# Products that nobody reads, issued in TensorE's waits at the end of a two-layer transformer block

## The chip, the cores and the metric

The kernel runs on one core of a Trainium2 chip. The metric is the device time of one execution in microseconds (us), the median of several runs. A core has a matrix engine (TensorE, PE in the profile; its weight loads stand apart as PEld), VectorE (DVE), ScalarE (ACT), GpSimd (POOL) and SyncE (SP, which issues most DMAs). Each engine works through its own list of instructions in order and waits on semaphores for the others. The profile also gives the TensorE clock that the chip granted, as a share of full speed.

## The reference

The input x is 2048 tokens of 256 values; a context of 1601 rows of 256 goes with it. Every step is added to x:

```python
x = x + cross_attention(layernorm(x), ctx, tau, delta)     # 16 heads of 16
x = x + experts(layernorm(x))                              # top 1 of 8, gated
x = x + local_attention(ctx, layernorm(x), slen, pt)       # a window around pt
x = x + slots(layernorm(x))                                # 64 slots
```

The last of them is what matters here. For every token it computes `h = gelu(x @ w1 + b1)`, logits over 64 slots, the 8 largest and a softmax over these (`alpha`). Then all tokens are summed into the slots (`slot_input = alpha.T @ x`, divided by the sum of alpha), a GRU cell updates the slots, they attend to each other, are normalized and projected, and `out = alpha @ slot_values` goes back to the tokens. So everything after `slot_input` needs all tokens, is small (64 rows), and is one chain.

## The kernel before

**Stages.** The first 820 us or so are the projections and the cross attention. Then come the experts in five blocks of tokens, `BLOCKS`: three of 512 tokens (four tiles of 128), two of 256. For each block, `experts(lb)` (line 1024 for the products, 1031 for VectorE's gated sums) is TensorE's main load. Beside it run generators, which are called a step at a time: `front(lb + 1)` (norm and router of the next block), `windowed(lb)` (the local attention of a finished block: lines 1179 to 1215) and `weights(lb)` (the slots' alpha of a finished block: lines 1297 to 1345). A `yield` ends a step, and the next step of another generator follows in the program.

**The order of work.** The order of instructions on every engine is the order in which the Python code emits them; the section is under `tc.manual_schedule()`, and no scheduler moves them. In the loop over blocks, `aside(3)` takes three steps of these generators behind each pair of experts. After the last block no experts are left, and

```python
    while beside:
        aside(1)
```

empties the generators that remain: the local attention and alpha of the last two blocks. This is called the flush here. What it emits: `normed` (L96 and L98 statistics on VectorE, L102 on GpSimd for 1/std, L107 the normalization, L984 transposes on TensorE, L987 copies on ScalarE), then for the window L1179 (`s_ps`), L1188 (exp), L1198 (`t_ps`), L1207 and L1211 (`o_ps`), L1213 (tanh), L1215 (the sum into x, on GpSimd); for the weights L1292 (a bias into x, on GpSimd), L1297 (`h_ps`), L1299 (gelu), L1303 (`l_ps`), L1307 to L1328 (logits, the 8 largest, softmax, alpha, nearly all on VectorE), L1335 (`si_ps`, the sum into the slots), L1341 (`at_ps`, alpha turned), L1343 and L1345 (its two parts `aT`).

**The slots' chain** follows the flush: L1390 to L1393 (`den`, `si`), L1399 (`siT`, turned), L1419 (`rz_ps` and `in_ps`), L1423 to L1434 (gates, tanh, the new state `sn`), L1399 (`snT`), L1442 and L1448 (q, k, v), L1452 (`qk_ps`), L1454 to L1461 (softmax), L1463 (`pt_ps`), L1467 (`sc_ps`), the norm (L96 to L107), L1399 (`yT`), L1475 and L1477 (`s_ps`), L1482 and L1483 (its two parts), and at last, for eight pairs of token tiles, L1492 (`f_ps`), L1498 (the sum `o`, on VectorE, three buffers) and L1499 (the DMA to the output).

**Products and records.** A float32 matmul stands in the trace as two records (two passes), a transpose, a float32r and a bfloat16 matmul as one. `xnT` is a float32 tile [128, 2, 512] that was last read by the experts of the first block. `y_pool` has four PSUM buffers, which the experts' products use in turn.

## Time and profile before

| what | value |
|---|---|
| median of 3 runs | 1109.17 us (1107.79 to 1112.33) |
| the profiled execution's own time | 1109.3 us |
| its span, first to last instruction | 1107.5 us |
| mean granted TensorE clock | 0.935 |
| TensorE busy | 970.1 us (88%) |
| VectorE busy | 744.4 us (67%) |
| ScalarE busy | 516.6 us (47%) |
| GpSimd busy | 71.9 us (6%) |

The span is what the trace covers; the execution's own time is 1.8 us longer. A busy time is the time in which an engine has at least one instruction in work. All positions in the text are us from the start of the span. The last expert product of the program ends near 1027, the flush reaches from about 1031 to 1071, the slots' chain from there to 1095, and the output to the end.

### The profile page before, as it was taken

Reading aid. Unit: us, or ns where it says so; the run is one execution under the profiler, and the core shown is the slowest. Engines: PE = TensorE matmul, PEld = TensorE weight load, DVE = VectorE, ACT = ScalarE, POOL = GpSimd, SP = SyncE. Lnnn points to the kernel's source line nnn. Section 1 sums busy time; section 2 is a strip of 40 time slices with the busy share of each in tenths; the row PEclk is TensorE's granted clock in tenths of the full one; section 3 lists DMA queues with packets and bytes.
Section 4 is the critical chain, followed back from the end, with each engine's and each line's share of the span. In section 5 each row is a group of like instructions: output and inputs, shape, how many; then the busy total and the mean of one; then the engine's idle time right before and its main releaser. Section 6 shows DMA issues by size and latency. Waiting matters only on the chain.

```text
span 1107.5 us, 14588 instructions
## 1 busy us (share of the span) xinstructions
PE 970.1 (88%) x5647; PEld 445.1 (40%) x5647; DVE 744.4 (67%) x1431; ACT 516.6 (47%) x614; POOL 71.9 (6%) x96
## 2 busy tenths in 40 slices
PE   5787879999888999988899999989979999989755
PEld 2243323344333344443344444344334454545523
DVE  6455857888676888776788877867025658586644
ACT  2323545666555666655466675656830012121420
POOL 4001100000010000000000000000030002111210
PEclk9676989999999999999999999989998999999767
DMA  4845630310103000102110010100051000000002
GB/s 167 171 120 115 118 113 1 104 28 1 27 2 112 28 1 27 28 1 70 43 28 23 6 28 1 27 2 1 2 168 51 1 1 1 0 1 1 1 0 76
DMA packets 32275, 46.95 MB, mean 42 GB/s; under 512 B 6411, under 2 KB 21268, under 8 KB 31950
## 3 DMA queue, kind: packets, MB, share of 16 engines
q1 hardware_dynamic: 30478, 43.65, 14.8%
q10 hardware_dynamic: 1232, 1.61, 0.4%
q8 instruction: 44, 0.72, 0.3%
q0 software_dynamic: 496, 0.76, 0.3%
q14 instruction: 25, 0.20, 0.1%
HBM read 26.77 MB, written 14.04 MB: 37 GB/s over the span
## 4 chain that ended last, share of the span: by engine, by line
PE 63%; DVE 27%; issue 5%; DMA 2%; ACT 1%; SPq 1%; POOL 1%; POOLq 0%; DVEq 0%; ACTq 0%
PE acc L832 18%; DVE mx L267 16%; PE a_ps L263 11%; PE s_ps L876 11%; PE y_ps L1024 6%; PE a_ps L240 2%; DVE xn L107 2%; DVE x_sb L1031 2%; DVE ln_stats L96 1%; PE a_ps L807 1%; PE o_ps L1207 1%; PE a_ps L510 1%; PE a_ps L293 1%; PE x_ps L473 1%; PE si_ps L1335 1%
## 5 line engine op out<-in xcount | busy, mean ns | idle before, releaser
L267 DVE TENSOR_REDUCE mx<-a_ps 128x1 f32<-128x402 f32 (+1 forms) x661 | 489.1, 782 | 130.5 <-PE a_ps L263 126.0
L881 ACT ACTIVATE es<-s_ps 128x1024 f32<-128x1024 f32 (+1 forms) x416 | 406.0, 1021 | 249.8 <-PE s_ps L876 230.0
L263 PE MATMUL a_ps<-kb,qb 50*128 50x402 bf16 x992 | 214.6, 347 | 35.2 <-DVE mx L267 12.0
L876 PE MATMUL s_ps<-qt,kt 52*128 52x512 f32 (+1 forms) x832 | 233.1, 518 | 2.1 <-DMA qt<-nT 2.1
L832 PE MATMUL acc<-es,v 128*32 128x512 f32 (+1 forms) x1664 | 229.8, 624 | 0.0
L263 PEld LDWEIGHTS <-qb 50*128 50x128 bf16 x1024 | 75.8, 95 | 300.3 <-issue 283.1
L876 PE MATMUL s_ps<-ql,kt 52*128 52x512 f32 (+1 forms) x832 | 187.6, 400 | 0.0
L876 PEld LDWEIGHTS s_ps<-qt,kt 52*128 52x128 f32 (+1 forms) x832 | 89.2, 187 | 50.4 <-ACT es L881 27.3
L876 PEld LDWEIGHTS s_ps<-ql,kt 52*128 52x128 f32 (+1 forms) x832 | 99.3, 189 | 0.4
L1024 PE MATMUL y_ps<-expert_wT_sb,xT 128*128 128x512 f32 x192 | 90.7, 605 | 0.0
L1031 DVE SCALAR_TENSOR_TENSOR x_sb<-y_ps,r_gate,x_sb 128x256 f32<-128x256 f32 x96 | 46.3, 482 | 32.9 <-PE y_ps L1024 31.2
L102 POOL TENSOR_TENSOR ln_rstd<-ln_ve,mhalf 128x2 f32<-128x2 f32 (+2 forms) x28 | 21.1, 754 | 714.5 <-DVE ln_ve L100 714.5
L832 PEld LDWEIGHTS acc<-es,v 128*32 128x32 f32 (+1 forms) x1664 | 33.3, 109 | 49.7 <-issue 48.1
L1024 PEld LDWEIGHTS y_ps<-expert_wT_sb,xT 128*128 128x128 f32 x192 | 34.6, 192 | 32.4 <-issue 30.8
L987 ACT COPY xT<-tr_ps 128x512 f32<-128x512 f32 (+1 forms) x28 | 13.5, 493 | 61.2 <-PE tr_ps L984 61.1
L781 DVE RECIPROCAL rec<-a_ps 128x16 f32<-128x16 f32 x16 | 4.1, 258 | 52.0 <-PE a_ps L240 52.0
L107 DVE TENSOR_SCALAR xn<-x_sb,ln_mv,ln_rstd 128x256 f32<-128x256 f32 x64 | 31.6, 539 | 1.1 <-POOL ln_rstd L102 1.1
L1024 PE MATMUL y_ps<-expert_wT_sb,xnT 128*128 128x512 f32 x64 | 32.0, 623 | 0.0
L984 PE MATMUL tr_ps<-ident,xn 128*128 128x128 f32 x88 | 17.8, 303 | 9.6 <-DVE xn L107 9.6
L1031 DVE SCALAR_TENSOR_TENSOR x_sb<-y_ps,gate,x_sb 128x256 f32<-128x256 f32 x32 | 15.5, 483 | 14.0 <-PE y_ps L1024 13.4
L96 DVE BATCH_NORM_STATS2 ln_stats<-x_sb 128x6 f32<-128x256 f32 x64 | 23.4, 413 | 1.8 <-POOL x_sb L1215 1.8
L267 DVE TENSOR_REDUCE mx<-s_ps 128x2 f32<-128x804 f32 x16 | 15.9, 994 | 12.5 <-PE s_ps L263 12.5
(341 smaller groups left out, 710.5 us busy)
## 6 DMA issues: line engine op xcount, KB each, us to landing
qt<-q_rows SPq DMA_DIRECT2D x32, 192.0 KB
q_rows<-qhi SPq DMA_DIRECT2D x8, 512.0 KB
qb<-q_rows SPq DMA_DIRECT2D x30, 96.0 KB
kt<-expert_wT_sb SPq DMA_DIRECT2D x24, 100.5 KB
q_rows<-qp SPq DMA_DIRECT2D x8, 256.0 KB
q_rows<-qlo SPq DMA_DIRECT2D x8, 256.0 KB
ql<-q_rows SPq DMA_DIRECT2D x32, 64.0 KB
expert_wT_sb<-in_expert_wT SPq DMA_DIRECT2D x1, 2048.0 KB
```

The costliest lines, as they stand in the source:

```text
L96: nc.vector.bn_stats(stats[:rows, i, :], src[:, i, :])
L102: nc.gpsimd.tensor_tensor(rstd[:rows, :n], ve[:rows, :n], mhalf[:rows, :n], ALU.pow)
L107: nc.vector.tensor_scalar(dst[:, i, :], src[:, i, :], mv[:rows, i, 0:1], rstd[:rows, i : i + 1], ALU.subtract, ALU.mult,)
L240: nc.tensor.transpose(ps[:, t * P : (t + 1) * P], src[:, t, c * P : c * P + n], ident)
L263: nc.tensor.matmul(ps[:, k, :CH], qb[u % 2][rows, pl, t * P : (t + 1) * P], kb[g][rows, pl, c * CH : (c + 1) * CH], start=True, stop=True,)
L267: nc.vector.tensor_reduce(flat[:, n : n + m], ps[:, :m, :CH], AX.X, ALU.max)
L832: nc.tensor.matmul(acc[HP * j : HP * (j + 1), :], v[:n, i, h * VW : h * VW + HP], es[j // 2][:n, j % 2, :], start=i == 0, stop=i == NS - 1,)
L876: nc.tensor.matmul(ps[:n, h, :], kt[u % NG][rows, pl, i * P : i * P + n], q[u % nq][rows, pl, :], start=k == 0, stop=k == 1,)
L881: nc.scalar.activation(e[:n], ps[:n], AF.Exp)
L984: nc.tensor.transpose(ps[:, t * P : (t + 1) * P], xn[:, t, c * P : (c + 1) * P], ident)
L1024: nc.tensor.matmul(ps.rearrange("p e d -> p (e d)"), xT[:, c, tok], ew[:, c, pair * 2 * D : (pair + 1) * 2 * D], start=c == 0, stop=c == 1,)
L1031: nc.vector.scalar_tensor_tensor(xb[:, t, :], ps[:, k, :], gate[:, t, e : e + 1], xb[:, t, :], ALU.mult, ALU.add,)
```

## The change

A helper `busy(n)` is added. It emits n bfloat16 products, each with its weight load: 128 columns of the upper halves of `xnT`'s float32 values as weights, 512 columns of such halves as the moving operand (every second bfloat16, thus a step of 4 bytes). All write the same PSUM tile, `busy_ps`, which nothing reads; none waits for another engine once that buffer is free. `busy` does nothing until `calm` holds that tile, and it gets it right before the flush. So products are emitted from there on alone: 95 of them, at places in `normed`, `windowed`, `weights` and the slots' chain. On TensorE they stand in the program's order: 8 ahead of the first `h_ps` and 6 behind it, 4 and 4 around the second transposes of the next blocks, 2, 4 and 3 around the next `s_ps` and `l_ps`, 4 ahead of `t_ps`, 4 ahead of `o_ps`, 8 behind it, 2 ahead of the last transposes, 2 ahead of the last `l_ps`, 12 behind it, 6 behind the last `at_ps`, 12 behind `in_ps`, 5 behind `qk_ps`, 9 behind `sc_ps`. All other instructions keep their order on every engine.

```diff
--- before
+++ after
@@ -961,6 +961,16 @@
     BLOCKS = [(0, TPB), (TPB, TPB), (2 * TPB, TPB), (3 * TPB, 2), (3 * TPB + 2, 2)]
 
+    calm = []
+
+    def busy(n):
+
+        for _ in range(n if calm else 0):
+            nc.tensor.matmul(
+                calm[0].rearrange("p e d -> p (e d)"), xnT[:, 1, :P].bitcast(BF16)[:, 1::2],
+                xnT[:, 0, :].bitcast(BF16)[:, 1::2], start=True, stop=True,
+            )
+
@@ -973,10 +983,12 @@
         for t in range(0, nt, 2):
             stats.append(layer_norm_stats(xb[:, t : t + 2], 2))
+            busy(4)
             yield
         for t in range(0, nt, 2):
             for k in range(2):
                 layer_norm_apply(xb[:, t : t + 2], xn[:, t : t + 2], k, stats[t // 2])
+            busy(2)
             yield
@@ -1192,6 +1204,7 @@
         nc.vector.tensor_tensor(sc, sc, sm.to_broadcast(full), ALU.mult)
+        busy(3)
         yield
@@ -1297,6 +1310,7 @@
         nc.scalar.activation(hT[:, : nt * P], ps, AF.Gelu, bias=b1)
+        busy(2)
         yield
@@ -1312,11 +1326,13 @@
             nc.vector.match_replace(rest[:, t, :], mx8[:, t, :], lg[:, t, :], -3e38)
+        busy(4)
         yield
 
         nc.vector.tensor_tensor(rest, rest, lg, ALU.not_equal)
         nc.vector.tensor_tensor(lg, lg, mx8[:, :, 0:1].to_broadcast(full), ALU.subtract)
         nc.scalar.activation(lg, lg, AF.Exp)
+        busy(4)
         yield
@@ -1329,6 +1345,7 @@
             sm.unsqueeze(2).to_broadcast(two_of), ALU.mult,
         )
+        busy(4)
         yield
@@ -1383,9 +1400,11 @@
+    calm.append(y_pool.tile([P, 2, D], F32, tag="y", name="busy_ps"))
     while beside:
         aside(1)
 
+    busy(6)
     den = slot.tile([NSLOT, 1], F32, name="den")
@@ -1419,6 +1438,7 @@
                 ps, siT[:, c, :], wih[:, c, span], start=c == 0, stop=c == 1
             )
+    busy(12)
     rz = brz
@@ -1450,6 +1470,7 @@
     nc.tensor.matmul(ps, qk[0], qk[1], start=True, stop=True)
+    busy(5)
     nmx = slot.tile([NSLOT, 1], F32, name="nmx4")
@@ -1465,6 +1486,7 @@
     nc.tensor.matmul(ps, paT, v4, start=True, stop=True)
+    busy(9)
     y = slot.tile([NSLOT, 1, D], F32, name="y4")
```

## The prediction

> **What bounds the kernel now.** I read the page's forty slices first, because the change adds work only at the end.

> ```profile
> PE 970.1 (88%) x5647; PEld 445.1 (40%) x5647; DVE 744.4 (67%) x1431; ACT 516.6 (47%) x614; POOL 71.9 (6%) x96
> ...
> PEclk9676989999999999999999999989998999999767
> ```

> TensorE is busy 88% of the span, but the last three slices (83 us) have a granted clock of 0.7, 0.6 and 0.7, where most others have 0.9 and more. Next I cut the end into stretches of 3.41 us, the grain in which the clock changes. Columns: stretch, length, busy us of PE, PEld, DVE, ACT and POOL with instructions, granted clock, DMA share, GB/s.

> ```profile
> 1031.22:1034.63 3.41, 2.54 (x10) 1.06 (x10) 3.05 (x12) 2.56 (x3) 1.69 (x3) 1.00 0.00 0
> 1034.63:1038.05 3.42, 1.36 (x11) 1.05 (x11) 3.16 (x4) 0.37 (x1) 3.42 (x3) 1.00 0.00 0
> 1038.05:1041.46 3.41, 2.47 (x9) 2.02 (x9) 3.20 (x14) 1.59 (x4) 0.85 (x1) 0.50 0.00 0
> ...
> 1048.29:1051.70 3.41, 3.41 (x12) 2.14 (x11) 0.67 (x5) 0.30 (x1) 0.00 (x0) 0.50 0.02 5
> 1051.70:1055.11 3.41, 2.75 (x14) 2.08 (x13) 2.45 (x7) 1.46 (x4) 0.00 (x0) 1.00 0.00 0
> 1055.11:1058.53 3.42, 1.41 (x6) 0.63 (x6) 1.20 (x6) 0.37 (x1) 1.97 (x2) 1.00 0.00 0
> 1058.53:1061.94 3.41, 2.91 (x8) 1.86 (x8) 1.10 (x3) 2.03 (x3) 1.27 (x1) 0.50 0.01 2
> ...
> 1079.01:1082.42 3.41, 0.31 (x2) 0.20 (x2) 2.33 (x7) 1.70 (x2) 0.00 (x0) 1.00 0.00 0
> 1082.42:1085.83 3.41, 3.22 (x14) 1.89 (x14) 1.05 (x5) 0.00 (x0) 0.00 (x0) 0.50 0.01 2
> 1085.83:1089.25 3.42, 0.88 (x3) 0.29 (x3) 1.78 (x7) 0.40 (x2) 0.00 (x0) 1.00 0.00 0
> ```

> Read each line's PE time against the clock of the *next*. At full clock, 2.75 of 3.41 (81%) and 2.54 (74%) keep it; 1.36 (40%), 1.41, 0.31 and 0.88 halve it. At half clock, 3.41 and 3.22 (94%) restore it; 2.47 (72%) and 2.91 (85%) don't. So 48 of the last 70 us run at half clock, after four waits. TensorE's waits of the end:

> ```profile
> PE tr_ps L984 <- DVE xn L107: 5.4, 3, 2.4
> PE si_ps L1335 <- DVE alpha L1328: 5.3, 3, 4.0
> PE snT_ps L1399 <- DVE sn L1434: 3.2, 1, 3.2
> PE l_ps L1303 <- ACT hT L1299: 2.5, 3, 1.1
> PE yT_ps L1399 <- DVE y L107: 2.5, 1, 2.5
> ```

> (Total us, times, longest.) TensorE waits for a chain over VectorE, ScalarE and GpSimd, then works slowly itself while they wait. The same `si_ps` matmuls in the timeline (start, us):

> ```profile
> 1055.07 1.08 PE L1335 MATMUL si_ps<-xn,alpha 128*64 128x257 f32 x4 [0.66 <-DVE alpha L1328]
> 1068.06 1.97 PE L1335 MATMUL si_ps<-xn,alpha 128*64 128x257 f32 x4 [4.05 <-DVE alpha L1328]
> ```

> Four records take 1.08 us at full clock and 1.97 at half.

> [...]the line lies between 41% and 74% here. [...]The trace has no such product. Its nearest row is the float32r `f_ps` (L1492), which reads 4 bytes per column as the strided product does: its 256 columns start 0.213 us apart at half clock and 0.113 to 0.123 at full, [...]a step of 4 bytes is no obstacle. [...]I take **0.216 us** a product; the lower end is 0.213, the upper 0.43[...].

> **The change, part by part.** Nothing is removed or moved, no DMA is added and no other engine's list changes; a product waits for nobody. Its cost is what it holds up on TensorE; its gain is the clock. If no stretch falls to 41%, all of 1038 to 1099 runs at full clock.

> Costs and gains along the path, before minus after:

> - 1031 to 1046.6. The 14 products around the first `h_ps` (3.0 us) make `l_ps` end near 1037.5 instead of 1035.5. Its reader, L1307, stands behind the normalization L107, which crawls beside GpSimd's L1292 until 1039.06: hidden. From 1039.11 to 1043.87 the PE work halves (4.76 to about 2.4) and takes in ten products (2.2): even. `l_ps` then waits for gelu, behind two table loads (cover for the next four), and alpha is VectorE's (cover for three): **0**.
> - 1046.63 to 1051.70 is PE work without a wait at half clock: 5.07 becomes 2.54, plus the eight products around `t_ps`, 1.73, which nothing hides: **0.8**.
> - Eight products behind `o_ps` end near 1055.3; alpha's `si_ps` starts 0.25 late, ends with `at_ps` and two more products near 1057.2, before `xn` at about 1057.7: **0**, beside tanh, L1215, the statistics and L102.
> - `tr_ps` to `h_ps`, 1.32 to 1.07: **0.25**. `h_ps` to gelu 2.11; afterwards the table load ends last, 0.31 + 1.28 behind `h_ps`' start: 1.6, **0.5**. `l_ps` to L1307, 1.15 to 0.64: **0.5** (the two products lie under gelu).
> - The twelve behind `l_ps`, 2.6 us, lie under VectorE's 4 us to alpha: **0**. `si_ps`, `at_ps`, L1343, L1345 to `den` took 3.47; the two PE parts lose 0.95 and 0.35: **1.3**. The six (1.3) lie under L1343 to L1393 (wait 1.8): **0**.
> - `siT`: **0.1**. `rz_ps` 3.67 to 1.85: **1.8**. L1427 waited for `in_ps` until 1079.06, 2.05 behind L1423; then for the sigmoid, 1.4: **0.6**. The twelve (2.6) lie under the gates, 3.2 before `snT`: **0**.
> - `snT` was at full clock. q, k, v and `qk_ps`, 3.2 to 1.85: **1.35**. Five products, 1.1, under the softmax's 1.4; nine, 1.94, under the norm's 2.5: **0**.
> - `yT` and `s_ps`, 1090.87 to 1094.47, 3.6 to 1.95: **1.65**. First `f_ps` group to `o`, 1.53 to 1.05, then VectorE's 0.69 a group and the output's 2.2 us DMA set the pace: **0.6**.

> Sum 0.8 + 0.25 + 0.5 + 0.5 + 1.3 + 0.1 + 1.8 + 0.6 + 1.35 + 1.65 + 0.6 = 9.45 us. From the profiled execution's 1109.3 (span 1107.5 and 1.8 around it; 0.13 above the median of 1109.17) that leaves 1099.85, so 1099.7 for the median. I say **1100.0**.

> **Rivals.**

> *The clock still drops once or twice.* The thinnest stretches left are those with `si_ps` and the transposes before 1060 (I count about 53% busy) and the one after 1037. Against: 53% lies above every stretch that dropped in the end of before. For: between 41% and 74% the lines above tell nothing. A drop costs half of 3.4 us of path work, 1.7, plus its products at twice the length, some 0.7. One or two take 2.4 to 4.8 from the gain: about 1103.

> *Slower: the products outlast the waits.* One mechanism: a product takes 0.43 us, because the strided read needs two cycles or because the clock isn't lifted by them. With the clock lifted, the flush's beginning then overruns its cover: 14 products are 6 us, and the eight between the transposes 3.4 where 2.4 were freed, about 4 us late at alpha. Add 3.4 around `t_ps`, and overruns of 1.1 (12 in 4.05), 0.8 (6 in 1.8), 1.9 (12 in 3.2), 0.7 (5 in 1.4) and 1.3 (9 in 2.5): 13.2. Against this stands a gain of 9.45 + 1.73 = 11.2: 2 us slower, 1111. If the clock isn't lifted at all, the cost is about 7 with no gain: 1116. The sign turns near 0.4 us a product. The `f_ps` starts speak against the first form; every restored stretch in the lines above having been full of real products speaks against the second.

> *No difference.* The clock is set by something else in this stage[...], or the products are undone. Their place in TensorE's list is that of the source, so the change does what it says; 1109.

> **How the numbers follow.** Forecast 0.58, dropped clock 0.22, no difference 0.10, slower 0.10. A measurement of this kernel tells about 0.5% (5.5 us) from no change, so faster means below 1103.6: the forecast and half of the dropped clock, 0.69, rounded to 0.70; same is the other half and no difference, 0.21, rounded to 0.20; slower 0.10. The range runs from 1097.5 (products that cost nothing around `t_ps`, 1.7 more gain, and rounding) to 1107, which takes in two or three drops; the other cases, 0.2, lie outside.

> **What would show it.** The clock is 1.00 in every stretch from 1031 to the output's start. `rz_ps` takes 1.9 us instead of 3.67, its neighbours likewise. The product's row has starts 0.216 apart and about 20 us in all. TensorE's waits before `si_ps`, `snT` and `yT` shrink to under 1.5 us and still end with VectorE; where the releaser of real work becomes a product, my covers are wrong. Starts 0.43 apart at clock 1.00 would make the slower rival true, a clock of 0.50 beside products the second form of it.

## The result

The changed kernel takes 1104.24 us (median of 20 runs, 1097.44 to 1108.69) against 1112.61 us (20 runs, 1107.58 to 1122.07) for the kernel before on the same chip. The ratio is **0.9918, 95% interval 0.9896 to 0.9939**. The forecast, 9.45 us of 1109.3, is a ratio of 0.9915. The kernel is faster, by as much as was said. In microseconds it lies above the forecast of 1100.0, mostly because the kernel before took 1112.61 here and not the 1109.17 that the forecast started from.

The page of the changed kernel answers the two lines shown of before. First TensorE's busy time and its number of matmuls, then the granted clock in forty slices:

```profile
PE 981.9 (89%) x5738; PEld 446.6 (40%) x5742; DVE 744.5 (67%) x1431; ACT 516.6 (47%) x614; POOL 71.9 (7%) x96
...
PEclk8676898999999999999999999998998989999999
```

The last three slices stand at 0.9 now. The trace holds 91 records of the 95 products; VectorE, ScalarE and GpSimd do the same work as before.

The profiled span is only 2.5 us shorter (1105.0 instead of 1107.5), because in that execution the flush began 6.44 us later, at 1037.56 instead of 1031.12. The part ahead of it is the same code in both, but spent a different time at half clock: 95.6 us ahead of the flush in the trace before, 109.2 in the trace of the changed kernel. So I compare the **tail**, from the flush's first `tr_ps` to the end of the last `o`: 72.95 us before, 64.02 after, 8.93 less. The tails of all kernels below are measured this way.

The stretches of 3.41 us that answer to those of before (stretch, length, busy us of PE, PEld, DVE, ACT and POOL with instructions, granted clock, DMA share, GB/s):

```profile
1037.13:1040.54 3.41, 3.35 (x16) 1.82 (x16) 2.53 (x10) 2.01 (x3) 1.84 (x2) 1.00 0.00 0
...
1043.96:1047.37 3.41, 2.29 (x14) 1.28 (x13) 3.27 (x11) 1.03 (x4) 1.44 (x2) 1.00 0.00 0
...
1071.26:1074.67 3.41, 2.08 (x10) 1.02 (x10) 1.23 (x5) 0.55 (x3) 0.00 (x0) 1.00 0.00 0
...
1081.50:1084.91 3.41, 2.48 (x18) 1.27 (x16) 1.92 (x6) 1.13 (x1) 0.00 (x0) 1.00 0.02 5
```

None of the stretches from here to the output's start is at 0.50. The thinnest has TensorE busy for 2.08 of 3.41 us (61%), around the wait for `alpha`, and keeps the clock. TensorE's longest waits of the end, in the changed kernel (total us, times, longest):

```profile
PE tr_ps L996 <- DVE xn L107: 2.1, 3, 1.0
PE si_ps L1352 <- DVE alpha L1344: 1.7, 2, 1.3
...
PE snT_ps L1418 <- DVE sn L1454: 0.5, 1, 0.5
...
PE yT_ps L1418 <- DVE y L107: 0.4, 1, 0.4
```

They are what is left behind the products: 4.0 became 1.3 before `si_ps`, 3.2 became 0.5 before `snT_ps`. The releaser is still VectorE, so the products lie under work that ended last anyway. The profile names a product as releaser once, for the weight load of the last `tr_ps` (1.5 us). That product ended near 1063.9 and the load started at 1064.84, and the transpose's own wait ends with `xn`, so no cover failed there. The timeline of TensorE shows it step by step (start, us, and in brackets the idle time ahead):

```profile
1068.51 2.88 PE L969 MATMUL busy_ps<-xnT 128*128 128x512 bf16 x12
1072.71 1.08 PE L1352 MATMUL si_ps<-xn,alpha 128*64 128x257 f32 x4 [1.33 <-DVE alpha L1344]
...
1076.67 1.93 PE L1438 MATMUL rz_ps<-WihT_sb,siT 128*64 128x512 f32 x4 [0.38 <-DVE siT L1423]
```

The last `si_ps` takes 1.08 us, where it took 1.97, and `rz_ps` 1.93, where it took 3.67.

### The profile page after: what moved, and what is told of

It is laid out like the page before. It is cut to its first block, busy times and chain, and to the rows that moved or that the text cites. A ratio compares the mean times of both kernels' runs of the same rounds, so it can differ in the third digit from the quotient of the medians.

```text
span 1105.0 us, 14775 instructions
## 1 busy us (share of the span) xinstructions
PE 981.9 (89%) x5738; PEld 446.6 (40%) x5742; DVE 744.5 (67%) x1431; ACT 516.6 (47%) x614; POOL 71.9 (7%) x96
## 4 chain that ended last, share of the span: by engine, by line
PE 63%; DVE 28%; issue 4%; DMA 2%; ACT 1%; SPq 1%; POOL 1%; POOLq 0%; DVEq 0%; ACTq 0%
PE acc L832 19%; DVE mx L267 16%; PE a_ps L263 11%; PE s_ps L876 10%; PE y_ps L1036 7%; DVE xn L107 2%; DVE x_sb L1043 2%; PE a_ps L240 2%; PE a_ps L510 1%; DVE ln_stats L96 1%; PE a_ps L807 1%; PE o_ps L1220 1%; PE a_ps L293 1%; PE x_ps L473 1%; PE a_ps L473 1%
## 5 line engine op out<-in xcount | busy, mean ns | idle before, releaser
L102 POOL TENSOR_TENSOR ln_rstd<-ln_ve,mhalf 128x2 f32<-128x2 f32 (+2 forms) x28 | 21.1, 753 | 709.8 <-DVE ln_ve L100 709.8
L107 DVE TENSOR_SCALAR xn<-x_sb,ln_mv,ln_rstd 128x256 f32<-128x256 f32 x64 | 31.8, 543 | 1.1 <-POOL ln_rstd L102 1.1
L969 PE MATMUL busy_ps<-xnT 128*128 128x512 bf16 x91 | 23.5, 387 | 0.4 <-issue 0.2
```

Source lines behind the costliest of these rows:

```text
L107: nc.vector.tensor_scalar(dst[:, i, :], src[:, i, :], mv[:rows, i, 0:1], rstd[:rows, i : i + 1], ALU.subtract, ALU.mult,)
L969: nc.tensor.matmul(calm[0].rearrange("p e d -> p (e d)"), xnT[:, 1, :P].bitcast(BF16)[:, 1::2], xnT[:, 0, :].bitcast(BF16)[:, 1::2], start ...
```

## The experiments

Ten kernels were run. "Restored" means that the clock goes from half to full, "dropped" the other way. Where a ratio is given, it is to the kernel before on the same chip.

**Only the flush, and only the chain.** Is the gain a sum of local ones, or does the chain need the products of the flush to hand it a full clock? In flush_only the four calls of the chain, 32 products, go:

```
-    busy(6)
     den = slot.tile([NSLOT, 1], F32, name="den")
...
-    busy(12)
     rz = brz
...
-    busy(5)
     nmx = slot.tile([NSLOT, 1], F32, name="nmx4")
...
-    busy(9)
     y = slot.tile([NSLOT, 1, D], F32, name="y4")
```

In chain_only the list stays empty until the flush is over, so its 63 products go:

```
-    calm.append(y_pool.tile([P, 2, D], F32, tag="y", name="busy_ps"))
+    hold = (y_pool.tile([P, 2, D], F32, tag="y", name="busy_ps"))
     while beside:
         aside(1)

+    calm.append(hold)
     busy(6)
```

> The 63 products of the flush stay, the 32 of the slots' chain (6, 12, 5, 9) are left out. I measure the tail: from the start of the transposes ahead of the first h_ps of the flush to the end of the last sum o; it was 72.9 us in the profile before and 64.0 in the changed kernel's. Theory (a 3.4 us stretch that is about 40% busy halves the clock, one over 90% busy restores it): full clock through the flush, then it drops in the wait for snT (3.2 us without a product) or already at siT, and q, k, v and from yT to f_ps run at half clock: 1.35 + 1.65 + 0.5 us lost, tail 67.5, up to 70 if it drops at siT. Rival (each product helps only where it stands, so the chain's whole share goes): the stages from siT on lose all their 6.0 us, tail 70.0. Rival (the clock has nothing to do with it): clock pattern as in the profile before.

> The 32 products of the slots' chain stay, the 63 of the flush are left out. Theory: four half-clock stretches as before from about 1038 to 1051 and from 1058 on; the six products ahead of siT run at half clock, 2.6 us against a wait of 1.8, so siT comes 0.8 late, but they fill the array, and the clock is restored within one or two stretches, during rz_ps; from snT on all is at full clock. Gain 1.35 + 1.65 + 0.5 and about half of 2.4, less 0.8: tail about 69. Rival (each product helps only where it stands): all of the chain's 6.0 us, tail 66.9.

flush_only: tail 69.79, ratio 0.9982 (0.9965 to 1.0000). Its stages in the flush are those of the changed kernel within 0.05 us; from there on the clock drops. Its stretches at the beginning of the chain:

```profile
1067.29:1070.70 3.41, 1.24 (x7) 0.54 (x6) 1.50 (x5) 1.66 (x2) 0.00 (x0) 1.00 0.00 0
1070.70:1074.12 3.42, 3.42 (x5) 0.95 (x5) 0.00 (x0) 0.00 (x0) 0.00 (x0) 0.50 0.00 0
```

Without the six products the wait for `si` leaves TensorE busy for 36% of a stretch, and the next, which holds `rz_ps`, runs at half clock:

```profile
1069.84 0.34 PE L1417 MATMUL siT_ps<-ident,si 64*128 64x64 f32 x2 [1.79 <-DVE si L1411]
1070.56 3.56 PE L1437 MATMUL rz_ps<-WihT_sb,siT 128*64 128x512 f32 x4 [0.38 <-DVE siT L1422]
```

chain_only: tail 68.83, ratio 0.9963 (0.9943 to 0.9982). The flush is as before, and `siT` comes 0.07 us later than before; from `rz_ps` on, every stage has the changed kernel's length. The six products behind the last `si_ps` restored the clock, and I had the chain lose more of its gain. The tail hides that, because one output transfer came late in this trace. TensorE's last four matmuls waited for `o`, and `o` for the buffer of a transfer:

```profile
DVE o L1521 <- DMA out_x<-o: 4.3, 3, 2.1
```

The stage from the first `f_ps` to the end took 10.62 us instead of 8.63. Why that transfer was late stays open, and so does whether it is late in most executions: the ratio's interval allows a gain of 2.0 to 6.3 us, which holds both cases. Without its 2.0 us the tail is 66.8, as the rival had it. The tail of flush_only fits the upper end of the theory (70) as well as the rival (70.0), so it is chain_only that tells them apart. Each half brings what its own stages are worth: 3.2 us in flush_only, and in chain_only 4.1, or 6.1 without the late transfer; with that, 9.3 in two parts against 8.9 together. So the idea that the chain needs a full clock handed on from the flush falls: six products restored it here.

**Short products.** Are the products themselves what helps, as instructions in the list, or the work that they give TensorE? The same 95 products with 64 columns instead of 512:

```
-    calm[0].rearrange("p e d -> p (e d)"), xnT[:, 1, :P].bitcast(BF16)[:, 1::2],
-    xnT[:, 0, :].bitcast(BF16)[:, 1::2], start=True, stop=True,
+    calm[0].rearrange("p e d -> p (e d)")[:, :64], xnT[:, 1, :P].bitcast(BF16)[:, 1::2],
+    xnT[:, 0, :64].bitcast(BF16)[:, 1::2], start=True, stop=True,
```

> All 95 products stay at their places, with 64 columns of the moving operand instead of 512 (about 0.05 to 0.11 us each). Theory (share of busy time): the waits are filled to no more than a half of what they were, the long ones (before si_ps, snT, yT) stay under 41% busy, and the clock drops there: at least three half-clock stretches, tail 70 to 73. Rival (that TensorE gets an instruction now and then is enough): full clock throughout, tail 62 to 63, since the products that nothing hides cost less.

Tail 71.76, ratio 1.0000 (0.9979 to 1.0021). The products fill too little of the waits; the clock still drops, five times in the tail:

```profile
1041.52:1044.94 3.42, 3.42 (x18) 2.81 (x17) 2.69 (x15) 2.60 (x6) 0.00 (x0) 0.50 0.02 5
1044.94:1048.35 3.41, 1.53 (x17) 1.28 (x16) 2.54 (x8) 3.33 (x4) 0.00 (x0) 1.00 0.00 0
1048.35:1051.76 3.41, 3.40 (x8) 1.66 (x8) 2.17 (x12) 0.00 (x0) 0.00 (x0) 0.50 0.00 0
```

A full stretch at 0.50 (3.42 us busy) restored the clock, one that was 45% busy (1.53, with 17 matmuls) dropped it. So the number of instructions brought little: 1.2 us of the 8.9. Whether it is the time that they fill or the columns that they move, this run doesn't tell; one_row below adds the rows.

**Twice the products.** Do the waits have room, and does the cost come back where they have none?

```
-        for _ in range(n if calm else 0):
+        for _ in range(2 * n if calm else 0):
```

> Each place has twice the products (190). Tests the price of a product and the covers. Theory: full clock throughout; each place's second half at 0.226 us each is compared with the wait that the changed kernel's profile still shows there: about 4.9 us late at the second si_ps stage, 1.8 around t_ps, 1.3 behind o_ps, 1.4 at the twelve before si_ps, 0.9 at siT, 2.2 at snT, 0.9 at pt_ps, 1.65 at yT: 15 us in all, tail 79, slower than before by some 5 us. Rival (products give way to real work that is ready): tail 64 to 66.

Tail 77.95, ratio 1.0087 (1.0058 to 1.0117), no stretch at half clock. The stages that the forecast had covered are full now: the first, to `si_ps`, takes 20.10 us instead of 15.52, and that from `pt_ps` to `yT_ps` 5.28 instead of 3.70. The products didn't give way to real work. The tail's 5.0 us over before make a ratio of 1.0045; the rest up to the lower end of the interval, 1.4 us, lies ahead of the tail and is not explained.

**Half of the products.** Where is the line between too thin and thick enough?

```
-        for _ in range(n if calm else 0):
+        for _ in range(n // 2 if calm else 0):
```

> Each place has half its products (n // 2, 44 in all). A measure of where the clock gives way. Theory: the waits ahead of the last si_ps, of snT and of yT are then filled to about 40 to 55% of their stretches, which is the range in which nothing has been seen; I expect one to three half-clock stretches, tail 64 to 69. Should the clock stay full everywhere, the tail is 63.1 (four of the eight around t_ps are gone), and a share near 45% is enough. Rival (a wait of any length between products lets it drop): four half-clock stretches, tail 70 or more.

46 products were issued, not the 44 that were expected. In the one execution, the tail is 67.70, with three stretches of half clock (3.4, 6.8 and 10.2 us long). Of its stretches, two show the difference:

```profile
1056.71:1060.12 3.41, 2.01 (x9) 1.22 (x9) 1.16 (x3) 1.55 (x3) 1.86 (x2) 1.00 0.01 2
1063.53:1066.95 3.42, 1.21 (x6) 0.66 (x7) 1.65 (x6) 0.31 (x1) 0.00 (x0) 1.00 0.00 0
```

59% kept the clock, 35% dropped it, and so did the 45% of short64. But busy time draws no fixed line, as two stretches of the kernel before show, both ahead of the flush and each with the one behind it:

```profile
894.70:898.11 3.41, 3.41 (x30) 3.30 (x30) 1.43 (x6) 0.23 (x1) 0.00 (x0) 1.00 0.02 5
898.11:901.53 3.42, 3.42 (x5) 1.15 (x4) 1.50 (x4) 0.42 (x1) 0.00 (x0) 0.50 0.00 0
...
993.68:997.09 3.41, 1.56 (x5) 0.52 (x4) 3.10 (x13) 0.45 (x1) 0.00 (x0) 1.00 0.00 0
997.09:1000.50 3.41, 3.41 (x25) 2.68 (x24) 0.39 (x1) 0.59 (x1) 0.00 (x0) 1.00 0.00 0
```

A stretch that was busy throughout lost the clock; it held matmuls of all 128 rows, but mostly of 8 and 65 columns. One that was 46% busy kept it; it held matmuls of 512 and 257 columns.

**Without the eight products that nothing hides.** The forecast charged 1.73 us for the four and four products around `t_ps`. They are the 11th and 12th calls of the helper:

```
-    calm = []
+    calm, calls = [], []
...
-        for _ in range(n if calm else 0):
+        calls.extend(calm)
+        for _ in range(n if calm and len(calls) not in (11, 12) else 0):
```

> The eight products around t_ps (4 and 4), which nothing hid, are left out; the other 87 stay. Tail as measured so far: 72.9 before, 64.0 with the change. Theory: from si_ps to o_ps TensorE has work of its own without a wait, so the clock stays full without them and the stage from si_ps to the end of o_ps falls from 7.16 by 8 x 0.226 to 5.35 us; all other stages keep their lengths: tail 62.2, a ratio of about 0.990. Rival (they were needed to keep the clock): a half-clock stretch follows, tail 64 or more.

Tail 62.47. The stage from the first `si_ps` to the end of `o_ps` takes 5.48 us instead of 7.16, 1.68 for eight products, and the clock stays full there: the real work around them is dense enough. The ratio is 0.9910 (0.9879 to 0.9941), which the total can't tell from that of the change, 0.9918. One stretch at half clock appeared further on, where the changed kernel has none, and cost some 0.15 us:

```profile
1085.45:1088.86 3.41, 2.82 (x12) 1.80 (x13) 0.85 (x2) 0.37 (x1) 0.00 (x0) 1.00 0.00 0
1088.86:1092.27 3.41, 3.41 (x18) 3.41 (x17) 2.18 (x4) 0.00 (x0) 0.00 (x0) 0.50 0.43 140
```

By busy time this doesn't fit: 2.82 of 3.41 us is 83%. The stretch holds `yT_ps` (64 rows of contraction) and the first half of `s_ps` (1 row), which led to the question of rows below.

**Does the data matter, or the step of 4 bytes?** Both kernels read products from a plain bfloat16 tile with a step of 2 bytes, written once, after the second block; zeros fills it with 0, dense with a copy of `xnT`:

```
+    plain = xnT[:, 1, : LB // 2].bitcast(BF16)
...
+        if lb == 2:
+            nc.gpsimd.memset(plain, 0.0)      # zeros
+            nc.gpsimd.tensor_copy(plain, xnT[:, 0, :])   # dense
...
-    calm[0].rearrange("p e d -> p (e d)"), xnT[:, 1, :P].bitcast(BF16)[:, 1::2],
-    xnT[:, 0, :].bitcast(BF16)[:, 1::2], start=True, stop=True,
+    calm[0].rearrange("p e d -> p (e d)"), plain[:, :P],
+    plain, start=True, stop=True,
```

> The products multiply zeros by zeros (the second half of xnT is cleared by GpSimd after the second block, and read with a step of 2 bytes). Theory (busy time counts, whatever is multiplied): full clock throughout, tail 64.0. Rival (the clock follows [...]the data): the products count for little, half-clock stretches as in the profile before, and products of 0.43 us on the path, tail 75 to 80.

> The products read a bfloat16 copy of the same values with a step of 2 bytes instead of 4 (GpSimd makes the copy after the second block). Tests whether the 0.226 us between the starts of two products, against the 0.216 that I had taken, come from the step of 4 bytes. If so: 0.216 or less, tail about 63.9. If not (the load of the weights or a fixed part is it): 0.226 again, tail 64.0.

One execution each: tails of 63.78 and 63.77, at full clock throughout. Products of zeros held the clock as those of real data did. The products start 0.216 us apart in both, where those of the change start 0.226 apart. Both operands changed their step, so which of them costs the 0.010 is not shown. The durations of single records differ by nearly as much, 387 ns against 379 (times in ns: least, median, most). The lines are of the changed kernel, dense and one_row; most of the last one's records ran at half clock:

```profile
L969 PE MATMUL busy_ps<-xnT x91: 385/387/400, 1038.3 to 1089.7; 128*128 128x512 bf16 x91
```

```profile
L969 PE MATMUL busy_ps<-xnT x95: 376/379/391, 1034.1 to 1085.4; 128*128 128x512 bf16 x95
```

```profile
L969 PE MATMUL busy_ps<-xnT x95: 380/604/627, 1041.1 to 1116.7; 1*128 1x512 bf16 x95
```

**One row.** Does the clock follow TensorE's busy time, or the rows of the array in use? The products read a single partition and keep their 512 columns, so their time at full clock should be the same (the shortest record took 380 ns, against 385 with all rows):

```
-    calm[0].rearrange("p e d -> p (e d)"), xnT[:, 1, :P].bitcast(BF16)[:, 1::2],
-    xnT[:, 0, :].bitcast(BF16)[:, 1::2], start=True, stop=True,
+    calm[0].rearrange("p e d -> p (e d)"), xnT[:1, 1, :P].bitcast(BF16)[:, 1::2],
+    xnT[:1, 0, :].bitcast(BF16)[:, 1::2], start=True, stop=True,
```

> The 95 products of the change with one partition of contraction instead of 128; same columns, same places, so the same busy time. In two profiles (half, trimmed) the clock fell after a stretch that was 64% and 83% busy, and both stretches held matmuls of 64 rows or of one. Theory A (busy time alone counts): full clock, tail 64.0. Theory B (the rows of the array that are in use count): the products are hardly seen, half-clock stretches as before, products of 0.43 us on the path: tail 73 to 80.

One execution: tail 90.00, 1135.75 us. In the stretch of half clock that is the longest:

```profile
1071.00:1101.70 30.70, 30.23 (x71) 11.84 (x70) 7.68 (x28) 6.72 (x10) 3.23 (x3) 0.50 0.00 0
```

TensorE is busy for 30.23 of 30.70 us, and the clock stays at 0.50. In the kernel before, a stretch that was 94% busy with real matmuls restored it. So in this run being busy was not enough: with products of one row the clock stayed where it was. The loss was larger than either theory had it, because at half clock a product takes 0.43 us (eight from 1073.88 take 3.59 us, the last record's 0.6 included), and the products run over the waits that cover them in the changed kernel. This is the second form of the forecast's slower rival, a clock that the products don't lift.

**The products elsewhere.** The same treatment for the longest wait ahead of the flush: 50 products of 64 rows of output by 256 columns before `eT_ps`, into the bank of `si_ps` that is written anew later, on top of trimmed:

```
+        for _ in range(50):
+            nc.tensor.matmul(
+                psi[:, :D], xnT[:, 1, :NSLOT].bitcast(BF16)[:, 1::2],
+                xnT[:, 0, :D].bitcast(BF16)[:, 1::2], start=True, stop=True,
+            )
```

> As trimmed (no products around t_ps), and 50 products of 64 by 256 columns ahead of the first transposes of the window (eT_ps), into the bank of si_ps, which nobody uses yet. TensorE waits 6.3 to 6.6 us there for a gathered DMA in every profile so far, and the clock is at half for 6.8 us, of which 2.9 to 5.5 lie behind eT_ps. Theory: the wait is filled (50 x 0.11 = 5.5 us), the half-clock stretch is gone, and the experts behind it gain half of it: from the start of eT_ps to the first eb_ps 18.3 to 18.6 us instead of 20.0 to 21.3; tail 62.5 as in trimmed. Ratio to before 0.988. Rival (64 columns fill half of the array and count for half): the clock drops all the same, 20 to 21 us, ratio 0.990 as trimmed.

```profile
836.01 5.86 PE L1139 MATMUL si_ps<-xnT 128*64 128x256 bf16 x50
842.46 0.30 PE L1145 MATMUL eT_ps<-ident,ew_w 64*128 64x64 f32 x2 [0.59 <-DVE nout L1121]
```

The wait of 6.3 to 6.8 us in the other kernels became 0.59, and no stretch at half clock follows. From `eT_ps` to the first `eb_ps` it took 19.08 us, where the others took 20.0 to 21.3; the forecast had hoped for 18.3 to 18.6. With the tail at 62.34 the ratio is **0.9874 (0.9827 to 0.9920)**, 1099.69 us: the lowest of the study. Its interval overlaps those of trimmed and of the change, so that it is also faster than these rests on the traces, not on the totals.

## Why the prediction was right

*The clock is what the end lost, and the products restored it.* Shown: the clock is full in every stretch of the tail, short64 with the same number of instructions still has half-clock stretches and gains 1.2 us of the 8.9, and half and flush_only lose in the stages where they leave a thin stretch. One_row adds the counter-test: as many products with as many columns, but of one row, leave 71.7 of the tail's 90.0 us at half clock. What the forecast had too simply is the yardstick: it read the share of busy time, which sorted the stretches that it showed, but not all (46% keeps, 100% drops). That it came out right goes with the form of the products, 128 rows by 512 columns: with 64 columns (short64) the clock dropped five times, and with one row (one_row) it stayed at 0.50 for 30.70 us.

*The sum.* Stages of the tail from start to start, in us:

| stage | before | after | gain | forecast |
|---|---|---|---|---|
| first `tr_ps` to first `si_ps` | 15.51 | 15.52 | 0.0 | 0 |
| to the end of `o_ps` | 7.78 | 7.16 | 0.62 | 0.8 |
| to the last `tr_ps` | 4.53 | 4.63 | -0.10 | 0 |
| to `h_ps` | 1.32 | 1.08 | 0.24 | 0.25 |
| to `l_ps` | 2.64 | 2.06 | 0.58 | 0.5 |
| to `si_ps` | 5.16 | 4.70 | 0.46 | 0.5 |
| to `siT_ps` | 4.38 | 3.24 | 1.14 | 1.3 |
| to `rz_ps` | 0.86 | 0.72 | 0.14 | 0.1 |
| to `snT_ps` | 8.56 | 6.16 | 2.40 | 1.8 + 0.6 |
| to `pt_ps` | 5.31 | 3.96 | 1.35 | 1.35 |
| to `yT_ps` | 3.70 | 3.70 | 0.0 | 0 |
| to the first `f_ps` | 4.05 | 2.45 | 1.60 | 1.65 |
| to the end of `o` | 9.14 | 8.63 | 0.51 | 0.6 |
| sum of the rounded values | 72.94 | 64.01 | 8.93 | 9.45 |

Every term holds within 0.2 us. The covers that I costed at nothing are there: 15.51 against 15.52 in the first stage, 3.70 against 3.70 under the softmax and the norm. The first stage rests in part on L107 being slow beside GpSimd's L1292: two of its instructions took 2.43 and 1.35 us there before and 2.47 and 1.35 after, where the two ahead of them took 0.41 each. The doubled products show that this was not free by nature: the same stages grew by 4.6 and 1.6 us.

*What was mis-sized.* The 0.5 us between forecast and sum lies mainly in three terms: 0.18 in the stage with the eight products, 0.16 in the last `si_ps` to `siT_ps`, and 0.10 behind `o_ps`, where I had written 0. In the first it isn't the products: trimmed measured the eight at 1.68 us, where I had 1.73, and that nothing hides them held. What was too large is the gain of the clock there: without the eight the stage takes 5.48 instead of 7.78, 2.30 less, where I had halved 5.07 to gain 2.53. I had also taken 0.216 us a product, which the trace before doesn't show (its nearest figure is the 0.213 of `f_ps`, 256 columns at half clock), and read from the `f_ps` row that a step of 4 bytes is no obstacle; it costs 0.010 us a product here, which dense and zeros show by taking it away (0.08 us in this stage: 7.08 instead of 7.16). The second lies in the two parts of TensorE that the forecast had at 0.95 and 0.35: `at_ps` starts 1.02 us behind `si_ps` instead of 1.90, a gain of 0.88, and its reader on ScalarE 0.47 behind that instead of 0.73, a gain of 0.26. The third was not taken apart.

*The rivals.* The clock that still drops once or twice was the nearest: the thinnest stretch is 61% busy, and with half of the products it happened three times. I had placed it at the `si_ps` and transposes before 1060 with 53%; there the stretches are 69% (2.36 of 3.42 us) and more, and the 61% lies at the wait for the last `alpha`. The slower rival needed a product of 0.43 us or a clock that isn't lifted; neither came with 128 rows, and one_row has both. Its price of 7 us was too low, as the 17 us of one_row's tail say: at half clock for most of the tail, the products overrun nearly every cover. No difference is excluded by the interval.

## What to carry to other kernels

Where the end of a kernel is a chain over several engines with TensorE waiting in between, cut it into the stretches in which the clock changes (3.41 us here) and look at TensorE's work in each, busy time first and then columns and rows, against the clock of the next. If the clock halves behind the thin ones (41% and less in the end of the kernel before) and the work behind them is TensorE's, products into a dead bank inside the wait can return the half, as they did here. Give each wait just what ends before the wait's own releaser; take many rows and columns (128 by 512 held the clock here, one row or 64 columns didn't), and leave out the products where real work is already dense (eight cost 1.68 us around `t_ps`). Judge it by the tail, or another stretch with fixed ends, since a gain of less than 1% is near the variation of the part ahead.
